# The last layer of a four-layer kernel: the fourth head's weights are turned by TensorE and copied by ScalarE, and unread bf16 products are set ahead of other products

## The chip, the cores and the metric

The kernel runs on one core of a Trainium2 chip. The core has engines with instruction streams of their own: PE (TensorE, matrix products; its weight loads are listed as PEld), DVE (VectorE), ACT (ScalarE), POOL (GpSimd) and SP (SyncE, which issues most DMAs here). PE writes to PSUM banks; DVE and ACT read them. The metric is the device time of one execution in microseconds, as the median of several runs.

## The reference

The input is x of 4 sequences by 1024 tokens by 128 features. Four layers each normalise x, apply a mixer and a feed-forward part, and add the product of the mixer's output and the silu of the other to x. Only the last layer's mixer matters here, attention with 16 heads of 8 features and learned relative distances:

```python
q, k, v = split_head(x @ Wq.T), split_head(x @ Wk.T), split_head(x @ Wv.T)
srel = srel_skew(einsum('bhnd,hmd->bhnm', q, e))      # e: embeddings by distance
qk = (einsum('bhnd,bhmd->bhnm', q, k) + srel) / sqrt(8)
atten = softmax(qk - mask)                             # causal
out = einsum('bhnm,bhmd->bhnd', atten, v) @ Wp.T + bp
```

With 1024 tokens and 256 embeddings, all farther distances share the first embedding. The feed-forward part of this layer is a gated one with 384 hidden features.

## The kernel before

`layer3` (L1736) holds the layer. Its 16 groups are 4 sequences by 4 sets i of 4 heads j. A group has 8 units, one for each tile t of 128 queries, in the order `ORDER3` = 7, 0, 6, 1, 5, 2, 4, 3 (L1733). A unit with tile t has (t + 1) x 128 keys, done in score tiles of up to 512 keys: one for t < 4, two for t > 3, so 12 score tiles a group and 192 in all.

**Scores** (`scores3`, L2077). The features of head j lie in rows 32j to 32j + 31, so a score product uses 32 of PE's 128 rows (L2097). Each score tile takes two PSUM tiles `halves`, heads 0 and 1 in one and heads 2 and 3 in the other, two banks each, from a pool of two such tiles (tag `sc`). DVE then reads them: it adds the distances `rel`, scales and finds the least value (L2113 for the up to five newest tiles of 128 keys, L2106 for older ones, where no distances are added), which frees the banks. ACT takes the exponential with the row's sum (L2120).

**Weights** (`transpose`, L1793). When all score tiles of a unit are compared, DVE turns the 4 heads' exponentials with a stream transpose (L1807), which turns each 32x32 block in its place, into `wT`. A unit with t > 3 is turned in two steps of two heads. Two units t = 2 pair and 2 pair + 1 share the buffers of a pair; there is one buffer for large t and one for small t, so that a new pair's transposes wait for the old pair's products.

**Weighted values** (`weigh3`, L2126). For blocks kb of 32 keys and each head, a product of `wT` with `vb` (L2134) adds to one PSUM tile `o`. Because of the 32x32 blocks, `vb` has the values placed so that each of four groups of 32 rows serves its own 32 queries. `values3` (L2009) loads the values in the layout of these blocks from DRAM, where `keep_values3` (L1886) put them, and POOL places them with four copies (L2018).

**Distances** (`relative3`, L2021). Two PSUM tiles `pr` for two heads take products of queries and embeddings (L2033); ACT copies them to `r` (L2035), and two DMAs on SP's queue write them to DRAM (L2038, L2039). `shear3` (L2042) reads them back shifted by row into `rel` and POOL masks them (L2064). The calls of `relative3` run 7 units ahead of their use, the reads about 3.

Beside it run, a step per unit, the feed-forward part (`ffn3`, L1972) of this sequence and the projections of the next sequence (`begin3`, L1933); the first sequence's are made during the third layer (`begin_first`, L1892). `finish3` (L2142) divides by the sums, `end3` (L2158) projects and stores. The tag `tr`, three banks, serves `pr`, `ffn3`, `begin3`, `finish3` and `end3`; tag `o` has one bank.

The program's main loop writes, for each score tile: the products of the next score tile, one waiting transpose, a step of the weighted values, the comparison of that next tile; and after a unit's last tile a call of `part` (distances), a step of project, of the parts beside, and `ahead` (the read of distances). A scheduler arranges each engine's instructions from this, by its own estimates, when the kernel is built; at run time each engine takes its own in order.

Of the kernel before, what the change touches and what calls it, by code (L numbers as in the profile page):

```python
# [10 lines left out]
F32 = mybir.dt.float32  # L11
BF16 = mybir.dt.bfloat16
# [8 lines left out]
P = 128  # L21
NB = 4
T = 1024
NT = 8
# [1711 lines left out]
def layer3(k, W, x3, out, eps5, ps, first):  # L1736
# [11 lines left out]
    nc, tc = k.nc, k.tc  # L1748
    with ExitStack() as st:
# [3 lines left out]
        for n in range(2):  # L1753
            q, kk = p1.tile([P, 1 + T], F32R, tag=f"q{n}", name="q"), p1.tile([P, T], F32R, tag=f"k{n}", name="k")
            nc.vector.memset(q[:, 0:1].bitcast(F32), 0.0)
            pairs.append((q, kk))
        vb = p1.tile([P, 32, 4, 4, 8], F32, tag="vb", name="vb")
        nc.gpsimd.memset(vb, 0.0)
        units = [(b, i, t) for b in range(NB) for i in range(4) for t in ORDER3]
        batch, group, flats, rels = {}, {}, {}, {}  # L1760

        def part(h):

            at, h = divmod(h, 8)
            if at < 4 * NB:
                pair = ORDER3[h // 4 * 4 + h // 2 % 2] // 2
                if h % 2 == 0:
                    flats[at, pair] = dram.tile([P, 4, 2, 384], F32, tag="flat", name="flat")
                relative3(k, W, temp, ps, flats[at, pair], group[at]["q"], at % 4, pair, h % 2)

        def ahead(n):
            if n < len(units):
# [2 lines left out]

        def stream():
            for n, (b, i, t) in enumerate(units):
                yield from scores3(k, p1, p2, ps, group[n // 8], rels.pop(n), t)

        batch[0] = {"qk": first["qk"], "vd": first["vd"], "xnT": p1.tile([P, T], F32, tag="xnT", name="xnT")}  # L1780
        nc.sync.dma_start(out=batch[0]["xnT"], in_=first["xnT"])
        group[0] = {}
        drain(project3(k, p2, pairs[0], batch[0], 0, group[0]))
        drain(values3(k, p1, batch[0], vb, 0))
# [8 lines left out]
        def transpose(n, heads):  # L1793

            b, i, t = units[n]
            at, pair = n // 8, t // 2
            big = t > 3
            if (at, pair) not in weights:
                for w in [w for w in weighs if w[0] == big]:
                    drain(w[1])  # L1800
                    weighs.remove(w)
                weights[at, pair] = [
                    p1.tile([P, 2, 1024 if big else 512], F32, tag=f"w{'b' if big else 's'}{j}", name="wT") for j in range(4)
                ]
            S = group[at]["S", t]
            for j in heads:
                nc.vector.transpose(weights[at, pair][j][:, t % 2, 0 : (t + 1) * P], S[j][:, 0 : (t + 1) * P])  # L1807
            if n % 8 in (2, 3, 6, 7) and heads[-1] == 3:
                weighs.append((big, weigh(n)))

# [28 lines left out]
        for x, (n, first) in enumerate(tiles + [(len(units), 0)] * 4):  # L1839
# [8 lines left out]
            b, i, t = units[n]  # L1848
# [34 lines left out]
        nc.sync.dma_start(out=rows[h], in_=a)  # L1883


def keep_values3(nc, to, v):  # L1886

    for a in range(4):
        nc.sync.dma_start(out=to[:, :, a], in_=v[32 * a : 32 * a + 32])


def begin_first(k, W, pool, ps, x, eps5, first):  # L1892
# [21 lines left out]
    for half in range(2):  # L1914
# [3 lines left out]
            nc.tensor.matmul(pv[:, t, :], xnT[:, at : at + P], W["WvT"], start=True, stop=True)  # L1918
        nc.scalar.copy(v[:, :, half * P : half * P + P].rearrange("p i (t d) -> p t i d", d=32), pv.rearrange("p t (i d) -> p t i d", d=32))
    keep_values3(nc, first["vd"], v)  # L1920
    yield


# [9 lines left out]
def begin3(k, W, p1, p2, temp, ps, dram, x3, b, eps5, seq):  # L1933
# [33 lines left out]
            yield  # L1967
    seq["vd"] = dram.tile([32, 4, 4, 256], F32, tag="vd", name="vd")
    keep_values3(nc, seq["vd"], v)


def ffn3(k, W, p1, temp, ps, seq):  # L1972
# [36 lines left out]
def values3(k, p1, seq, vb, i):  # L2009

    nc = k.nc
    v = p1.tile([P, 32, 32], F32, tag="vr", name="vr")
    at = seq["vd"][:, i]
    nc.sync.dma_start(out=v.rearrange("p n d -> p (n d)"), in_=bass.AP(at.tensor, at.offset, [(0, 4), (4096, 32), (1, 1024)]))
    yield
    for a in range(4):
        rows = slice(32 * a, 32 * a + 32)
        nc.gpsimd.tensor_copy(vb[rows, :, :, a, :], v[rows].rearrange("p n (j d) -> p n j d", d=8))  # L2018


def relative3(k, W, temp, ps, flat, q, i, pair, jp):  # L2021

# [2 lines left out]
    r = temp.tile([P, 2, 2, 256], F32, tag="temp", name="r")  # L2027
    js = (2 * jp, 2 * jp + 1)
    pr = [ps.tile([P, 2, 256], F32, tag="tr", name="pr") for _ in js]
    for m in range(2):  # L2030
        for j, to in zip(js, pr):
            at, t = slice(32 * j, 32 * j + 32), 2 * pair + m
            nc.tensor.matmul(to[:, m, :], q[at, t * P : (t + 1) * P], W["emb"][at, i, :], start=True, stop=True)  # L2033
# [40 lines left out]
    return rel  # L2074


def scores3(k, p1, p2, ps, group, rel, t):  # L2077

# [12 lines left out]
    for first in range(0, n, 512):  # L2093
        last = min(first + 512, n)
        halves = [ps.tile([P, 2, 512], F32, tag="sc", name="score") for _ in range(2)]
        for j in range(4):
            nc.tensor.matmul(  # L2097
                halves[j // 2][:, j % 2, 0 : last - first], q[at(j), 1 + t * P : 1 + n], kk[at(j), first:last], start=True, stop=True
            )
# [26 lines left out]
def weigh3(k, weights, vb, o, pair):  # L2126
# [4 lines left out]
    for n, kb in enumerate(groups):  # L2131
        m = slice(1, 2) if kb in second else slice(0, 2)
        for j in range(4):
            nc.tensor.matmul(  # L2134
                o[32 * j : 32 * j + 32, 2 * pair + m.start : 2 * pair + 2, :], vb[:, kb % 4 * NT + kb // 4, j].rearrange("p a d -> p (a d)"),
                weights[j][:, m, 32 * kb : 32 * kb + 32], start=(kb == 0), stop=(kb == both[-1]),
            )
        if pair > 1 and n + 1 in (len(groups) // 3, 2 * len(groups) // 3):
# [55 lines left out]
def tile_kernel(ctx: ExitStack, tc: tile.TileContext, I, out):  # L2194
# [9 lines left out]
    store = ctx.enter_context(tc.tile_pool(name="x3", bufs=1, space=DRAM))  # L2204
    x3 = store.tile([P, NB * NT, D], F32, tag="x3", name="x3")

    first = {name: store.tile(shape, F32, tag=name, name=name) for name, shape in (("qk", [2, 4, 4, 32, T]), ("vd", [32, 4, 4, 256]), ("xnT", [P, T]))}
    whole = ExitStack()
    xp = whole.enter_context(tc.tile_pool(name="x", bufs=1, side="right"))
    x_all = xp.tile([P, NB * NT, D], F32, tag="x_all", name="x_all")  # L2210
# [51 lines left out]
```

## Time and profile before

| | us |
|---|---|
| median of 3 runs (3174.36 to 3178.80) | 3178.16 |
| the profiled execution | 3175.99 |
| its span, first to last instruction | 3174.2 |
| first to last score product (the last layer's loop) | 985.5 |
| busy over the span: PE, DVE, ACT, POOL | 2163.6, 2291.8, 1542.6, 1167.5 |

A group's line names the line of the kernel, the engine, the operation, what it writes and reads, the shape and how often; then its busy time, the mean of one in ns, and after the bar the engine's idle time just before these instructions, with what ended it. A line of stretches gives a stretch of the span, then for each engine the busy time and the number of instructions in it, the mean granted TensorE clock (1 is full speed), the mean busy share of the 16 DMA engines, and GB/s. Matmuls are pipelined, so that the busy time of PE counts a product until its end, and products may overlap. Over the span's 40 slices the granted clock is 0.7 to 0.9 in the first eighteen, apart from one of 0.5, and 0.5 to 0.7 in the rest.

### The profile page before, as it was taken

How to read it: one execution, taken by the hardware profiler on the slowest of the kernel's cores; microseconds unless marked ns; L12 is line 12 of the kernel's file. 1: busy time of each engine (PE TensorE's matmuls, PEld its weight loads, DVE VectorE, ACT ScalarE, POOL GpSimd, SP SyncE). 2: the span in 40 equal slices, each digit the busy share in tenths (PEclk: the TensorE clock that was granted, in tenths of full speed). 3: DMA queues.
4: the chain of work that ended last, by engine and by line, in shares of the span. 5: the costliest groups of instructions: out<-in, count | busy, mean ns of one | idle time of the engine just before them, and what ended most of it. 6: DMA issues, size and time to landing. Idle time of an engine off the chain costs nothing. (4 is left out here: it accounts for less than half of the span.)

```text
span 3174.2 us, 47753 instructions
## 1 busy us (share of the span) xinstructions
PE 2163.6 (68%) x17039; PEld 1256.8 (40%) x17041; DVE 2291.8 (72%) x5558; ACT 1542.6 (49%) x3300; POOL 1167.5 (37%) x1094
## 2 busy tenths in 40 slices
PE   5777777577887776794543574375777777777865
PEld 2555555232332232562210122253544544544543
DVE  5554544878888786656778888676788797687777
ACT  3554544333333333535432463145765775775773
POOL 3433444144444434123477433232333332323322
PEclk9888888588888887895655566565766666766666
DMA  3000000100000000230334356339588588678772
GB/s 78 16 1 1 1 1 1 35 0 0 0 0 0 7 7 7 103 110 20 74 92 114 123 120 136 100 118 295 174 256 272 176 268 261 197 242 269 215 242 66
DMA packets 334065, 333.13 MB, mean 105 GB/s; under 512 B 25968, under 2 KB 307436, under 8 KB 328196
## 3 DMA queue, kind: packets, MB, share of 16 engines
q1 hardware_dynamic: 332676, 325.90, 34.6%
q10 hardware_dynamic: 1152, 4.19, 0.4%
q8 instruction: 134, 2.20, 0.3%
q14 instruction: 103, 0.84, 0.1%
HBM read 175.31 MB, written 154.14 MB: 104 GB/s over the span
## 5 line engine op out<-in xcount | busy, mean ns | idle before, releaser
L2120 ACT ACTIVATE neg<-neg,low 128x640 f32<-128x640 f32 (+7 forms) x512 | 390.7, 766 | 105.8 <-DVE low L2113 104.6
L1807 DVE STREAM_TRANSPOSE wT<-neg 128x640 f32<-128x640 f32 (+7 forms) x512 | 366.3, 754 | 50.3 <-PE po L2134 45.5
L2064 POOL TENSOR_SCALAR_AFFINE_SELECT rel<-rel 128x512 f32<-128x512 f32 x288 | 180.5, 638 | 551.4 <-DMA rel<-flat 412.6
L2134 PE MATMUL po<-wT,vb 128*32 128x64 f32 (+1 forms) x10240 | 266.2, 253 | 71.9 <-issue 40.8
L2097 PE MATMUL score<-k,q 32*128 32x512 f32 (+3 forms) x768 | 220.5, 587 | 124.6 <-DVE low L2113 121.3
L2134 PEld LDWEIGHTS po<-wT,vb 128*32 128x32 f32 x10240 | 210.9, 134 | 144.5 <-issue 84.1
L2113 DVE CUSTOM_DVE_ANT_0 neg<-score,rel,low 128x128 f32<-128x128 f32 (+3 forms) x448 | 213.0, 510 | 71.4 <-PE score L2097 29.3
L2035 ACT COPY r<-pr 128x512 f32<-128x512 f32 x256 | 135.2, 584 | 126.4 <-PE pr L2033 79.8
L2113 DVE CUSTOM_DVE_ANT_0 neg<-score,rel 128x512 f32<-128x512 f32 (+3 forms) x320 | 150.6, 520 | 50.4 <-POOL rel L2064 21.2
L2097 PEld LDWEIGHTS score<-k,q 32*128 32x128 f32 x768 | 96.8, 247 | 214.1 <-DVE low L2113 139.6
L837 PE MATMUL pg<-xnT,w 128*128 128x512 f32 x256 | 149.1, 666 | 7.1 <-DVE h L841 4.0
L2033 PE MATMUL pr<-emb,q 32*128 32x256 f32 x512 | 125.8, 426 | 39.7 <-ACT r L2035 25.5
L840 ACT ACTIVATE h<-pg 128x512 f32<-128x512 f32 x128 | 75.9, 596 | 157.5 <-PE pg L837 154.1
L790 POOL TENSOR_TENSOR prod<-rest,kv 128x2048 f32<-128x2048 f32 x32 | 145.5, 4598 | 18.4 <-ACT rest L780 18.4
L839 PE MATMUL pu<-xin,w 128*128 128x512 f32 x256 | 140.5, 632 | 12.9 <-DVE h L841 7.4
L828 PE MATMUL po<-h,w 128*128 128x512 f32 x256 | 129.8, 628 | 26.5 <-DVE h L841 26.5
L216 PE MATMUL pt<-ident,three 128*24 128x128 bf16 x64 | 9.2, 295 | 196.6 <-DVE three L213 196.6
L2033 PEld LDWEIGHTS pr<-emb,q 32*128 32x128 f32 x512 | 89.0, 262 | 74.4 <-ACT r L2035 38.9
L433 PE MATMUL px<-hT,xbcT 128*128 128x512 f32 x256 | 115.0, 593 | 0.0
L1086 PE MATMUL ph<-xin,upT 128*128 128x512 bf16 (+1 forms) x126 | 68.3, 572 | 66.4 <-DVE xin L1080 64.0
L1491 PE MATMUL read<-kt,const_sb 128*128 128x128 f32 x256 | 51.1, 372 | 90.3 <-POOL kt L1486 90.3
L785 DVE TENSOR_REDUCE s<-prod 128x128 f32<-128x2048 f32 x32 | 73.1, 2284 | 49.6 <-POOL prod L790 49.6
(633 smaller groups left out, 5775.7 us busy)
## 6 DMA issues: line engine op xcount, KB each, us to landing
flat<-r SPq DMA_DIRECT2D x128, 512.0 KB
rel<-flat SPq DMA_DIRECT2D x112, 512.0 KB
flat<-r SPq DMA_DIRECT2D x128, 256.0 KB
rel<-flat SPq DMA_DIRECT2D x96, 256.0 KB
kt<-kd SPq DMA_DIRECT2D x16, 512.0 KB
qt<-qd SPq DMA_DIRECT2D x16, 512.0 KB
kdc<-kdd SPq DMA_DIRECT2D x16, 512.0 KB
ktc<-ktd SPq DMA_DIRECT2D x16, 512.0 KB
```

The costliest lines, as they stand in the source:

```text
L790: nc.gpsimd.tensor_tensor(prod, attn.rearrange("p (t h g) -> p t h g", t=4, g=16)[:, t].unsqueeze(2).to_broadcast(each), kv[:, t, 1, :].re ...
L828: nc.tensor.matmul(po, W["w2"][:, e, c, :], h[:, c, :], start=(e == 0 and c == 0), stop=(e == 7 and c == 1))
L837: nc.tensor.matmul(pg, W["w1"][:, e, c * P : (c + 1) * P], xnT, start=True, stop=True)
L839: nc.tensor.matmul(pu, W["w3"][:, e, c * P : (c + 1) * P], xin, start=True, stop=True)
L1807: nc.vector.transpose(weights[at, pair][j][:, t % 2, 0 : (t + 1) * P], S[j][:, 0 : (t + 1) * P])
L2033: nc.tensor.matmul(to[:, m, :], q[at, t * P : (t + 1) * P], W["emb"][at, i, :], start=True, stop=True)
L2035: nc.scalar.copy(r[:, n], to)
L2064: nc.gpsimd.affine_select(out=rel[:, :, slot(back), :], in_=rel[:, :, slot(0), :], compare_op=op, fill=fill, base=0, pattern=[[0, 4], [-si ...
L2097: nc.tensor.matmul(halves[j // 2][:, j % 2, 0 : last - first], q[at(j), 1 + t * P : 1 + n], kk[at(j), first:last], start=True, stop=True)
L2113: nc.vector.tensor_tensor_reduce(out=neg[:, begin:last], in0=sc[:, begin - first : last - first], in1=rel[:, j, slot : slot + (last - begi ...
L2120: nc.scalar.activation(neg[:, 0:n], neg[:, 0:n], AF.Exp, bias=here, scale=-1.0, accum_out=group["sums"][:, j, t : t + 1])
L2134: nc.tensor.matmul(o[32 * j : 32 * j + 32, 2 * pair + m.start : 2 * pair + 2, :], vb[:, kb % 4 * NT + kb // 4, j].rearrange("p a d -> p (a ...
```

## The change

For j < 3 nothing changes in the transposes. For j = 3, PE transposes blocks of 128x128 (f32, by the identity) into a PSUM tile of tag `tr`, up to four blocks in one, and ACT copies that tile to `wT`. Since these blocks are turned whole, the fourth head's values need another placing: a second tile `vc` of 128 keys by block, query quarter and head feature, filled from `v3`, which for the first sequence goes through DRAM and for the others is copied by POOL. `vb` shrinks from four to three heads. The number and shapes of products in `weigh3` stay.

`beat` is a product of the bf16 identity with a tile of bf16 ones, 128x512, into a bank that the next real product writes anew, so that nothing reads it. It is set ahead of each half of a score tile (heads 0 and heads 2) and, in `relative3`, once for each of the two banks `pr`.

```diff
-        vb = p1.tile([P, 32, 4, 4, 8], F32, tag="vb", name="vb")
-        nc.gpsimd.memset(vb, 0.0)
+        vb = (
+            p1.tile([P, 32, 3, 4, 8], F32, tag="vb", name="vb"), p1.tile([P, NT, 4, 4, 8], F32, tag="vc", name="vc"),
+        )
+        for a in vb:
+            nc.gpsimd.memset(a, 0.0)
+        ones = p1.tile([P, 512], BF16, tag="ones16", name="ones")
+        nc.gpsimd.memset(ones, 1.0)
+
+        def beat(bank):
+            nc.tensor.matmul(bank, k.ident16, ones, start=True, stop=True)
...
+        batch[0]["v3"] = p2.tile([P, 4, NT, 8], F32, tag="v3", name="v3")
+        nc.sync.dma_start(out=batch[0]["v3"], in_=first["v3"])
...
             for j in heads:
-                nc.vector.transpose(weights[at, pair][j][:, t % 2, 0 : (t + 1) * P], S[j][:, 0 : (t + 1) * P])
+                to = weights[at, pair][j][:, t % 2]
+                if j < 3:
+                    nc.vector.transpose(to[:, 0 : (t + 1) * P], S[j][:, 0 : (t + 1) * P])
+                    continue
+                for begin in range(0, t + 1, 4):
+                    end = min(begin + 4, t + 1)
+                    pt = ps.tile([P, 4, P], F32, tag="tr", name="pt")
+                    for c in range(begin, end):
+                        nc.tensor.transpose(pt[:, c - begin, :], S[j][:, c * P : (c + 1) * P], k.ident)
+                    nc.scalar.copy(to[:, begin * P : end * P], pt[:, 0 : end - begin, :].rearrange("p c q -> p (c q)"))
...
+def fourth(v):
+    return v.rearrange("p i (t d) -> p i t d", d=32)[:, :, :, 24:32]
...  (begin_first)
+    nc.sync.dma_start(out=first["v3"], in_=fourth(v))
...  (begin3)
+    seq["v3"] = p2.tile([P, 4, NT, 8], F32, tag="v3", name="v3")
+    nc.gpsimd.tensor_copy(seq["v3"], fourth(v))
...  (values3)
-        nc.gpsimd.tensor_copy(vb[rows, :, :, a, :], v[rows].rearrange("p n (j d) -> p n j d", d=8))
+        nc.gpsimd.tensor_copy(vb[0][rows, :, :, a, :], v[rows].rearrange("p n (j d) -> p n j d", d=8)[:, :, 0:3])
+    for a in range(4):
+        nc.gpsimd.tensor_copy(vb[1][:, :, a, a, :], seq["v3"][:, i])
...  (relative3)
     pr = [ps.tile([P, 2, 256], F32, tag="tr", name="pr") for _ in js]
+    for to in pr:
+        beat(to.rearrange("p m u -> p (m u)"))
...  (scores3)
         for j in range(4):
+            if j % 2 == 0:
+                beat(halves[j // 2][:, 0])
             nc.tensor.matmul(
...  (weigh3)
-                o[32 * j : 32 * j + 32, 2 * pair + m.start : 2 * pair + 2, :], vb[:, kb % 4 * NT + kb // 4, j].rearrange("p a d -> p (a d)"),
+                o[32 * j : 32 * j + 32, 2 * pair + m.start : 2 * pair + 2, :],
+                (vb[0][:, kb % 4 * NT + kb // 4, j] if j < 3 else vb[1][:, kb // 4, kb % 4]).rearrange("p a d -> p (a d)"),
```

## The prediction

> **What bounds the kernel now.** I read the page's slices first, then the totals of the last layer's loop, then that loop in stretches of 10 us, then the waits of its lines, and last the granted clock window by window. The change touches the last layer alone; its loop of 192 score tiles runs from 2155.1 us to 3140.6 us, 985.5 us of the span of 3174.2 us.
>
> The totals of that loop (columns: busy time and instructions of each engine, mean granted TensorE clock, DMA share, GB/s):
>
> ```profile
> 2155.10:3140.60 985.50, 723.21 (x11750) 483.75 (x11750) 779.97 (x2535) 672.47 (x1512) 308.13 (x412) 0.68 0.76 233
> ```
>
> No engine is full: PE 73%, DVE 79%, ACT 68%, and the clock averages 0.68. The 10 us stretches show why; four of them:
>
> ```profile
> 2550.00:2560.00 10.00, 6.67 (x124) 4.16 (x120) 9.82 (x33) 4.97 (x10) 6.64 (x8) 0.90 1.08 372
> 2560.00:2570.00 10.00, 4.46 (x16) 2.04 (x16) 10.00 (x41) 4.61 (x14) 1.84 (x3) 0.50 1.02 294
> 2570.00:2580.00 10.00, 9.72 (x275) 7.69 (x279) 7.71 (x35) 9.31 (x18) 2.19 (x5) 0.58 0.71 194
> 2510.00:2520.00 10.00, 7.05 (x207) 5.53 (x205) 3.31 (x12) 9.88 (x18) 3.53 (x6) 1.00 0.70 202
> ```
>
> The lead changes. I took the busiest engine of each of the 97 stretches from 2160 us on. DVE leads in 52 (mean busy DVE 9.41, ACT 6.93, PE 6.70 us; clock 0.65), PE in 33 (6.09, 5.97, 8.28; 0.69), ACT in 12 (6.58, 9.09, 7.67; 0.76). The waits, by line, tie PE and DVE together:
>
> ```profile
> L1807 DVE STREAM_TRANSPOSE wT<-neg 128x640 f32<-128x640 f32 (+7 forms) x512 | 366.3, 754 | 50.3 <-PE po L2134 45.5
> L2097 PE MATMUL score<-k,q 32*128 32x512 f32 (+3 forms) x768 | 220.5, 587 | 124.6 <-DVE low L2113 121.3
> L2035 ACT COPY r<-pr 128x512 f32<-128x512 f32 x256 | 135.2, 584 | 126.4 <-PE pr L2033 79.8
> ```
>
> DVE spends 366 us turning weights, and waits 45.5 us there for the products that still read the old ones; PE waits 121 us for DVE to release score banks.
>
> The clock's record takes only the values 0.5 and 1.0 and changes at multiples of 3.41 us. Two successive windows, two more, and two from layer 2:
>
> ```profile
> 2503.37:2506.79 3.42, 3.42 (x21) 2.17 (x23) 1.35 (x7) 1.98 (x7) 1.57 (x3) 0.50 0.58 190
> 2506.79:2510.20 3.41, 3.41 (x53) 2.60 (x41) 1.72 (x7) 3.38 (x4) 0.73 (x1) 1.00 0.43 117
> 2517.03:2520.44 3.41, 0.11 (x2) 0.09 (x1) 0.55 (x2) 3.36 (x5) 2.11 (x4) 1.00 1.01 326
> 2520.44:2523.85 3.41, 3.41 (x17) 2.39 (x17) 0.00 (x0) 0.34 (x1) 1.23 (x2) 0.50 0.02 4
> ...
> 1547.64:1551.05 3.41, 3.19 (x14) 2.79 (x15) 0.50 0.85 202
> 1551.05:1554.46 3.41, 2.99 (x12) 0.89 (x10) 1.97 (x3) 2.97 (x7) 2.09 (x7) 1.00 0.69 147
> ```
>
> A window with much array work is followed by the full clock, one with little by half. For each window of the loop I counted columns streamed, an f32 column as two and a bf16 column as one (128 f32 columns start 111 ns apart at full clock, 512 bf16 columns 215 ns), times the share of array columns used, and left out products with 32 rows. Of 184 windows under 2,500, 6 were followed by full clock; of 74 at 3,000 or more, all. In the loop 33% of windows reach 2,600 and 36% run at full clock.
>
> **The change, part by part.** The sum is made against the profiled execution, 3175.99 us, 2.2 us below the median of 3178.16 us.
>
> *Transposes off DVE.* One of four per unit, 128 in all. The eight widths average 276 to 1232 ns and add to 6.03 us per group; 16 groups give 96.5 us, 12.4% of DVE's 780. In a DVE-led stretch that is 9.41 to 8.25 us.
>
> *Copies on ACT.* 192: 96 of 128x512 at 584 ns (the copy of products with distances), 32 each of 128, 256 and 384 columns. 256 columns took 376 ns (the copy of a group's output); the line through both gives 272 and 480. Sum 56.1 + 36.1 = 92 us, 13.7% of ACT's 672. In a DVE-led stretch ACT goes from 6.93 to 7.9 us, still below DVE; in an ACT-led one it adds up to 1.25 us where 0.91 is idle: +8 us over 12 stretches, between 0 and 15.
>
> *Transposes on PE.* 36 per group, 576. f32 transposes start 213 ns apart at half clock, 109 at full: 123 or 63 us.
>
> *Unread products.* Two per score tile (384) and two per call for distances (256): 640, each with its weight load. Nearest rows: bf16 128x512 with loads between, 308 to 320 ns apart at full and 537 at half; with loads hidden (24 rows), 215. So 138 to 202 us at full, up to 344 at half. A load needs no bank and may go ahead during the wait, which argues for the low end; I take the middle: 232 us for both additions at full clock, 2.36 us per 10 us.
>
> *The clock.* The products add 640 x 512 and the transposes 576 x 256 columns-worth, spread over 284 windows: 1,155 + 520. Added evenly, 62% of windows reach 2,600 instead of 33%. I take 0.70 of the time at full clock, since a PE with little idle time leaves fewer thin windows; the bounds are 0.45 (bunched, or PE waiting) and 0.85.
>
> [...] The window from 1547.64 us above holds 14 f32 transposes and hardly anything else, and the next ran at 1.00, so here they count. [...]
>
> *PE's sum.* At half clock the same work runs at 0.56 of full rate (109/213 for transposes, 493/791 for score products, medians). DVE-led: 6.70 us at 30% full is 4.64 us of full-clock work; the additions, in proportion to DVE's work (9.41 to a mean of 7.91), 2.8. Together 7.45, and at 0.70 full (rate 0.868) 8.58 us. That is above DVE's 8.25, so PE leads; with the 0.59 us idle of today's leader a stretch takes 9.17 instead of 10: 52 x 0.83 = -43 us. PE-led: 8.28 at 38% full is 6.02; additions 1.82; 9.03 us at the new clock, 0.75 more, of which I let half disappear in the 1.72 us idle: 33 x 0.37 = +12 us.
>
> *Waits.* The turned tiles use the three banks that products with distances also use, 12 more tiles a group beside their 16. PE waits for ACT's copies there about 0.15 us a bank today (25.5 us in 256 products' banks by the matmuls, 38.9 by the loads); 192 more give 29 us of PE wait, of which the PE-led third shows, +8. Queued behind that wait are the next score products, and DVE behind them; DVE's transposes cover it, and if they did not all 29 would show. On ACT the new copies wait for PE; the next unit's exponentials queue behind. The 45.5 us that DVE waits for old weights, the 51 for scores and 18 for the sums' product shrink with a faster PE: about -10, bounded by 0 and -20.
>
> *Edits at about nothing.* POOL fills two value tiles: four copies of 32x768 and four of 128x64 for four of 32x1024 (1,034 ns each), between -1 and +3 us a group. POOL is busy 31% and waits 412.6 us for distances to land; were that cover gone, it would be up to 48 us. One store (32-byte runs), one load and one fill at the layer's start, the load ahead of q and k on SP's queue: +1. No DMA is added per group.
>
> Sum: -43 + 12 + 8 + 8 - 10 + 1 = -24 us, about 0.8%; on the median some 3154 us.
>
> **Rivals.** (1) *The clock stays low and PE becomes the bound* (slower). For: full clock needs each window to be dense, and the unread products wait for the same bank as the scores, so they cannot fill PE's 121 us of waiting for DVE. Against: 62%. At 0.52 full (rate 0.789) DVE-led stretches take 9.44 + 0.59, +2 us in all; PE-led 9.94, of whose 1.66 more three quarters show, +41; with the +17 of the rest about +60 and, less the shrinking waits, 3178 + 55. It decides at 0.62 full, a granted clock of 0.81, where the sum is zero. (2) *Loads hide and the clock holds* (faster by more). At 0.85 full and 200 us of additions, PE needs 7.6 us in DVE-led stretches, so DVE's 8.25 leads: 8.84, -60; PE-led -6; the rest +7: 3119. For: once full, windows of 3,000 kept it in 52 of 52. Against: PE starves whenever DVE holds the banks. (3) *ACT or the landing of distances takes DVE's place* (no change): every DVE-led stretch stays at 10 us and only small terms remain, 3178 within 6 us. Against: ACT 7.9, DMA share 0.76.
>
> **How the numbers follow.** Forecast, 6 to 45 us faster: 0.38. Rival 2, more than that: 0.18. No change (0.2% is 6 us, about what a measurement of this kernel can tell): 0.08. Rival 1: 0.36. Faster 0.56, same 0.08, slower 0.36. The likeliest case alone spans 3133 to 3172. The range for 8 in 10 runs from 3100 (past rival 2, with ACT's +8 at zero and the waits at -20) to 3230 (rival 1).
>
> **What would show it.** Right: the loop's granted clock above 0.81; STREAM_TRANSPOSE x384 and about 96 us less DVE time; some 192 copies of about 480 ns on ACT; unread products 215 to 320 ns apart at full clock; DVE's wait for old weights below 45 us. Wrong: a clock under 0.8 with PE above 90% busy; exponentials waiting for PE's transposes; PE waiting for ACT's copies much beyond 60 us; DVE waiting longer for scores than 51 us.

## The result, and the profile after

The changed kernel takes 3289.59 us (median of 4 runs, 3287.22 to 3292.09) against 3178.36 us for the kernel before in the same session: ratio 1.0353, 95% interval 1.0335 to 1.0371. It is 111 us slower. I had forecast 3154 us. Nearly all of the difference lies in the last layer's loop, which grew from 985.5 to 1098.2 us; it starts 4 us later.

The loop in one stretch, first to last score product (as before: length, then busy time and instructions of PE, PE's loads, DVE, ACT and POOL, granted TensorE clock, DMA share, GB/s):

```profile
2159.50:3257.70 1098.20, 960.37 (x12940) 562.86 (x12939) 713.65 (x2410) 740.18 (x1690) 306.41 (x474) 0.79 0.69 208
```

PE is busy 960 us in place of 723, DVE 714 in place of 780, ACT 740 in place of 672. The clock rose from 0.68 to 0.79. Since the record holds only 0.5 and 1.0, that is 58% of the time at full clock in place of 36%. So the clock did rise and DVE was relieved; but only PE has less idle time in the loop than before, and DVE's went from 205 to 385 us.

The groups of the changed kernel (line, engine, operation, tiles, shapes, count; busy us, mean ns of one; idle time before them and its main cause):

```profile
L2154 ACT ACTIVATE neg<-neg,low 128x640 f32<-128x640 f32 (+7 forms) x512 | 391.8, 770 | 33.8 <-DVE low L2147 33.1
...
L2147 DVE CUSTOM_DVE_ANT_0 neg<-score,rel,low 128x128 f32<-128x128 f32 (+3 forms) x448 | 215.8, 515 | 150.2 <-PE score L2131 105.8
L1821 DVE STREAM_TRANSPOSE wT<-neg 128x1024 f32<-128x1024 f32 (+7 forms) x384 | 276.5, 756 | 56.0 <-PE po L2168 47.9
...
L1767 PE MATMUL score<-ones,ident 128*128 128x512 bf16 x384 | 179.0, 466 | 36.1 <-DVE low L2147 35.3
...
L1767 PE MATMUL pr<-ones,ident 128*128 128x512 bf16 x256 | 107.8, 464 | 30.3 <-ACT r L2067 17.3
L1828 ACT COPY wT<-pt 128x384 f32<-128x384 f32 (+1 forms) x192 | 86.7, 479 | 72.1 <-PE pt L1827 71.9
```

The prices of the moved work came out near my own: DVE's transposes fell from 366.3 to 276.5 us (-90; I had 96.5), ACT's 192 copies take 86.7 us at 479 ns (I had 92 and about 480). The unread products did not: the mean record is 466 ns. The comparison's line (L2113 before, L2147 after) tells what happened to DVE: 71.4 us of idle time before it became 150.2, led by PE's scores, 29.3 before and 105.8 now. The line before:

```profile
L2113 DVE CUSTOM_DVE_ANT_0 neg<-score,rel,low 128x128 f32<-128x128 f32 (+3 forms) x448 | 213.0, 510 | 71.4 <-PE score L2097 29.3
```

The same loop by waits (engine and line that waited, for whom; us in total, times, longest):

```profile
PEld score L2131 <- issue: 148.3, 373, 4.1
DVE neg L2147 <- PE score L2131: 128.6, 84, 11.2
ACT r L2067 <- PE pr L2065: 121.1, 62, 21.2
...
ACT wT L1828 <- PE pt L1827: 71.9, 76, 5.7
...
DVE neg L2140 <- PE score L2131: 51.1, 31, 15.1
...
DVE wT L1821 <- PE po L2168: 47.9, 18, 7.1
...
DVE neg L2147 <- ACT neg L2154: 39.5, 16, 4.7
...
PE score L1767 <- DVE low L2147: 35.3, 46, 3.6
...
DVE neg L2147 <- PE pt L1827: 22.9, 10, 4.8
```

The same waits in the kernel before:

```profile
PEld score L2097 <- issue: 58.1, 74, 2.1
...
DVE neg L2113 <- PE score L2097: 31.2, 23, 4.1
...
DVE neg L2106 <- PE score L2097: 20.1, 16, 9.3
```

DVE waits 180 us for scores (128.6 + 51.1; before 31.2 + 20.1). Before, PE waited 121 us for DVE to free score banks; now 35, and it is the unread product that waits. The score products wait instead behind it: their loads show 148 us of "issue", where no other engine holds them, 373 times (58 us and 74 times before). The 45.5 us that DVE waited for old weights did not shrink (47.9).

A stretch of the timeline shows the unread product in DVE's path (start, duration, engine, instruction, and in brackets the idle time before it with its cause):

```profile
2551.76 0.61 PE L1767 MATMUL score<-ones,ident 128*128 128x512 bf16 x1
...
2552.09 0.08 DVE L2140 DVE_READ_ACCUMULATOR neg<-score 128x1 f32 x1
2552.30 0.29 PEld L2131 LDWEIGHTS score<-k,q 32*128 32x128 f32 x2 [0.43 <-issue]
2552.30 0.79 PE L2131 MATMUL score<-k,q 32*128 32x512 f32 x2
...
2553.23 0.29 DVE L2140 TENSOR_SCALAR_CACHE_REDUCE neg<-score 128x128 f32<-128x128 f32 x1 [1.06 <-PE score L2131]
```

DVE is done at 2552.17 and has nothing to compare. PE starts the unread product at 2551.76, the load of the first score product only at 2552.30, and DVE starts at 2553.23, 1.06 us idle. The clock is at half here (0.50), as it mostly is when DVE waits for scores: of the 180 us, 109 lie in windows at half clock, which make up 42% of the loop.

### The profile page after: what moved, and what is told of

Its sections match the earlier page's. It is cut to its first block, busy times and chain, and to the rows that moved or that the text cites. A ratio compares the mean times of both kernels' runs of the same rounds, so it can differ in the third digit from the quotient of the medians.

```text
span 3290.4 us, 50230 instructions
## 1 busy us (share of the span) xinstructions
PE 2409.9 (73%) x18257; PEld 1338.7 (41%) x18257; DVE 2223.9 (68%) x5430; ACT 1613.2 (49%) x3484; POOL 1168.4 (36%) x1163
## 5 line engine op out<-in xcount | busy, mean ns | idle before, releaser
L2147 DVE CUSTOM_DVE_ANT_0 neg<-score,rel,low 128x128 f32<-128x128 f32 (+3 forms) x448 | 215.8, 515 | 150.2 <-PE score L2131 105.8
L1821 DVE STREAM_TRANSPOSE wT<-neg 128x1024 f32<-128x1024 f32 (+7 forms) x384 | 276.5, 756 | 56.0 <-PE po L2168 47.9
L2168 PE MATMUL po<-wT,vb 128*32 128x64 f32 (+1 forms) x7680 | 219.4, 238 | 28.8 <-issue 22.8
L2147 DVE CUSTOM_DVE_ANT_0 neg<-score,rel 128x512 f32<-128x512 f32 (+3 forms) x320 | 154.3, 523 | 111.7 <-ACT neg L2154 39.5
L1767 PE MATMUL score<-ones,ident 128*128 128x512 bf16 x384 | 179.0, 466 | 36.1 <-DVE low L2147 35.3
L2168 PEld LDWEIGHTS po<-wT,vb 128*32 128x32 f32 x7680 | 178.3, 124 | 64.4 <-issue 41.1
L2131 PE MATMUL score<-k,q 32*128 32x512 f32 (+3 forms) x768 | 203.4, 516 | 0.1
L2168 PE MATMUL po<-wT,vc 128*32 128x64 f32 (+1 forms) x2560 | 190.6, 238 | 9.1 <-issue 8.9
L2168 PEld LDWEIGHTS po<-wT,vc 128*32 128x32 f32 x2560 | 164.5, 124 | 22.2 <-issue 17.5
L1827 PE MATMUL pt<-const_sb,neg 128*128 128x128 f32 x576 | 125.2, 356 | 14.0 <-ACT neg L2154 5.9
L1767 PE MATMUL pr<-ones,ident 128*128 128x512 bf16 x256 | 107.8, 464 | 30.3 <-ACT r L2067 17.3
L1828 ACT COPY wT<-pt 128x384 f32<-128x384 f32 (+1 forms) x192 | 86.7, 479 | 72.1 <-PE pt L1827 71.9
```

Source lines behind the costliest of these rows:

```text
L1767: nc.tensor.matmul(bank, k.ident16, ones, start=True, stop=True)
L1821: nc.vector.transpose(to[:, 0 : (t + 1) * P], S[j][:, 0 : (t + 1) * P])
L2131: nc.tensor.matmul(halves[j // 2][:, j % 2, 0 : last - first], q[at(j), 1 + t * P : 1 + n], kk[at(j), first:last], start=True, stop=True)
L2147: nc.vector.tensor_tensor_reduce(out=neg[:, begin:last], in0=sc[:, begin - first : last - first], in1=rel[:, j, slot : slot + (last - begi ...
L2168: nc.tensor.matmul(o[32 * j : 32 * j + 32, 2 * pair + m.start : 2 * pair + 2, :], (vb[0][:, kb % 4 * NT + kb // 4, j] if j < 3 else vb[1][ ...
```

## The experiments

Eighteen kernels ran, in five sessions; each ratio is against the kernel before on the same chip. "Score wait" is DVE's wait for score products in the loop, "full" the share of the loop at full clock (twice the granted clock, less one).

| run | edit | us | ratio, 95% interval | loop us | full | PE, DVE busy us | score wait us |
|---|---|---|---|---|---|---|---|
| before | | 3178 | 1 | 985.5 | 0.36 | 723, 780 | 51 |
| after | the change | 3289.6 | 1.0353 (1.0335 to 1.0371) | 1098.2 | 0.58 | 960, 714 | 180 |
| e1 | after, no unread products | 3226.9 | 1.0149 (1.0119 to 1.0179) | 1041.2 | 0.37 | 813, 708 | 113 |
| e2 | before, with unread products | 3232.2 | 1.0168 (1.0137 to 1.0199) | 1039.6 | 0.52 | 919, 785 | 105 |
| e8 | e2 with 128 columns | 3217.4 | 1.0129 (1.0100 to 1.0158) | 1021.7 | 0.37 | 874, 785 | 88 |
| e5 | before, DVE relieved | 3150.2 | 0.9924 (0.9901 to 0.9946) | 964.8 | 0.33 | 729, 705 | 63 |
| e6 | before, with unread turns | 3187.5 | 1.0030 (1.0008 to 1.0051) | 1000.4 | 0.40 | 792, 784 | 59 |
| e7 | before, with unread copies | 3160.8 | 0.9949 (0.9934 to 0.9964) | 972.3 | 0.35 | 713, 781 | 34 |
| e10 | e5 and e6 | 3158.2 | 0.9933 (0.9914 to 0.9951) | 967.9 | 0.45 | 774, 707 | 71 |
| e13 | e10 and whole copies | 3203.6 | 1.0079 (1.0063 to 1.0095) | 1010.7 | 0.41 | 815, 711 | 75 |
| e14 | e1, copies unread | 3183.0 | 1.0020 (1.0008 to 1.0032) | 993.4 | 0.45 | 787, 708 | 67 |
| e16 | before, products bunched | 3211.6 | 1.0104 (1.0091 to 1.0117) | 1023.7 | 0.32 | 711, 782 | 61 |
| e17 | before, products spread | 3205.6 | 1.0080 (1.0067 to 1.0093) | 1021.5 | 0.33 | 737, 785 | 75 |
| e18 | e1, products lagging | 3242.4 | 1.0194 (1.0176 to 1.0213) | 1060.3 | 0.41 | 858, 713 | 118 |

**The two halves of the change.** e1 takes the two `beat` calls out of the changed kernel, e2 puts them alone into the kernel before.

```diff
# e1, against after
-    for to in pr:
-        beat(to.rearrange("p m u -> p (m u)"))
...
-            if j % 2 == 0:
-                beat(halves[j // 2][:, 0])
# e2, against before: the same four lines added, with ones and beat
```

> The changed kernel without its 640 unread products; the fourth head is still turned by PE and copied by ACT. Theory A (the unread products fill PE: they took 237 us of PE's own time in the loop of the changed kernel, and the faster clock gave back less): PE's time falls from 960 us to about 780, the loop's granted clock from 0.79 to about 0.72, DVE's wait for scores from 180 us to about 70, and the time is 3165 to 3215 us. Theory B (the turning on PE is what costs, by the shared banks and by ACT's queue): 3250 us or more, with DVE still waiting over 120 us for scores. Theory C (each part alone fits into PE's idle time, only both together fill it): 3185 us or less.

> The kernel before with the 640 unread products alone; DVE turns all four heads. Theory A: PE's time rises from 722 us to about 850, the granted clock from 0.68 to 0.76 or more, and the time is 3230 to 3290 us. Theory B: 3178 us or less, since the clock is faster and nothing else is in the way. Theory C: within 30 us above 3178.

Both halves lose on their own: the turning 48 us (3226.9 against 3179.2 in that session), the unread products 53, and their sum of 101 is near the 111 of both. The clock that the unread products bring is real (e2: 52% at full clock in place of 36%), but what it gives back is less than what they take. Counted from each product's start to the next start on PE (or to its own end, if PE is idle then), the unread products take 252 us of e2's loop, 0.40 us each, while all of PE's work together grew by 196 (722 to 918): the rest of it, at the faster clock, became 56 us shorter.

**Where the unread products stand.**

```diff
# e3, against after: ahead of score halves only
-    for to in pr:
-        beat(to.rearrange("p m u -> p (m u)"))
# e4, against after: ahead of products with distances only
-            if j % 2 == 0:
-                beat(halves[j // 2][:, 0])
```

> The changed kernel with the 384 unread products ahead of half score tiles alone, none ahead of products with distances. Theory A by PE time (150 of the 237 us): between the run without any and the changed kernel, nearer the latter: about 3250 us. If it is their place that matters, between DVE's release of the banks and the scores that DVE waits for: nearly all of the loss, 3275 us or more.

> The changed kernel with the 256 unread products ahead of products with distances alone. Theory A by PE time (87 of the 237 us): about 3225 us. If it is the place ahead of scores that matters: within 15 us of the run without any unread product.

e3 took 3256.2 us (1.0244, 1.0200 to 1.0288) and e4 3264.7 us (1.0271, 1.0230 to 1.0311). Above e1 that is 29 us for 384 products and 38 us for 256, together 67 where both at once cost 63. So no place among the two is harmless, and they add up. Those ahead of the distances look dearer, 0.148 us of time each against 0.076, but by two runs each, with intervals of some 14 us to either side.

**Array time or the mere instruction.**

```diff
# e8, against e2
-            nc.tensor.matmul(bank, k.ident16, ones, start=True, stop=True)
+            nc.tensor.matmul(bank[:, 0:128], k.ident16, ones[:, 0:128], start=True, stop=True)
```

> The kernel before with the 640 unread products ahead of the same products, each of 128 columns in place of 512. If their streaming time is what costs (0.40 us each with 512 columns in the run with unread products alone, 53 us slower): a quarter to a third of the loss, 3190 to 3200 us, and a granted clock of the loop near 0.70. If a weight load and an issue in front of the scores cost as much: 3215 us or more.

A quarter of the columns still costs 40 of e2's 53 us. The loop of e2 as one stretch, first to last score product, in the columns used above:

```profile
2159.56:3199.15 1039.59, 918.64 (x12373) 503.66 (x12372) 784.78 (x2536) 674.80 (x1510) 306.94 (x411) 0.76 0.71 219
```

And of e8:

```profile
2155.31:3177.01 1021.70, 873.95 (x12381) 557.58 (x12380) 784.83 (x2535) 677.06 (x1512) 307.92 (x412) 0.68 0.73 224
```

With 128 columns the clock is not lifted (0.68), and PE is still busy 874 us. By starts, the short products themselves take 117 us, the score products 212 in place of 188 and those with distances 136 in place of 104: at half clock one of the latter goes from 239 to 347 ns. The starts show where this comes from. Before, 1006 of the score and distance products, which use 32 rows each, are followed on PE by another of them, after 161 ns on average counted as above, and 503 of these starts come within 50 ns, where a score product's record lasts 587 ns on average: such products overlap. In e8, 365 of them are followed by an unread product, which uses all rows; it never starts sooner than 202 ns after, on average 431 ns. So the price is the interruption as much as the 512 columns, and it stays when the clock's gain is gone.

**The turning, part by part.** Unread transposes on PE, unread copies on ACT, and DVE relieved of its transposes with nothing in their place:

```diff
# e5, against before (fourth head's products read the third head's turned weights)
+                if j < 3:
+                    nc.vector.transpose(weights[at, pair][j][:, t % 2, 0 : (t + 1) * P], S[j][:, 0 : (t + 1) * P])
-                nc.vector.transpose(weights[at, pair][j][:, t % 2, 0 : (t + 1) * P], S[j][:, 0 : (t + 1) * P])
...
-                weights[j][:, m, 32 * kb : 32 * kb + 32], start=(kb == 0), stop=(kb == both[-1]),
+                weights[min(j, 2)][:, m, 32 * kb : 32 * kb + 32], start=(kb == 0), stop=(kb == both[-1]),
# e6, against before: for j == 3 also
+                    pt = ps.tile([P, 4, P], F32, tag="tr", name="pt")
+                    for c in range(begin, end):
+                        nc.tensor.transpose(pt[:, c - begin, :], S[j][:, c * P : (c + 1) * P], k.ident)
# e7, against before: for j == 3 also
+                    spare = p1.tile([P, 512], F32, tag="spare", name="spare")
+                    nc.scalar.copy(spare[:, 0 : (end - begin) * P], S[j][:, begin * P : end * P])
```

> The kernel before without the fourth head's stream transposes, and nothing in their place: the products with the fourth head's values read the third head's turned weights, so the fourth head's result is left out. This is the gain that was to be had from DVE alone. If DVE's own time bounds the loop, about 96 us less of it shows for the most part: 3090 to 3120 us. If the ties between PE and DVE bound it: 3130 us or more.

> The kernel before, and beside it PE transposes the fourth head's blocks (576 of them) into the same three banks, where nobody reads them; DVE still turns all four heads. This is the cost of PE's part alone. If scores queue behind PE's added time of some 130 us: 3225 us or more. If that time falls into PE's 263 us of waiting: 3190 us or less, and the loss of the turning lies with ACT's copies and the banks held for them.

> The kernel before, and beside it ACT copies the fourth head's exponentials to a spare tile that nobody reads, 192 copies of the same widths. This is the cost of ACT's part alone, about 90 us of ACT time. If ACT has room (it is busy 672 of 985 us): 3190 us or less. If exponentials and copies of distances queue behind: 3215 us or more.

Taking 75 us of work off DVE saved 27 (3150.2 against 3177.0). DVE's time without work in the loop grew from 205 to 260 us: the wait for POOL's distances from 44 to 63, for scores from 51 to 63. PE's transposes cost 10 us. ACT's copies cost less than nothing, -16: no work was taken away in e7, so this gain must come from how the rest is arranged by the build's scheduler and falls in time, which was not tried apart. The three sum to -33, while all of them together cost +48, with the link that the change has: the fourth head's products read ACT's copies and the second value tile. That gap of 81 us was the open question.

**Banks.** My first explanation was that turned tiles hold the three `tr` banks until ACT, in order behind its exponentials, copies them.

```diff
# e9, against e6: the bank is held until ACT gets to it
+                    spare = p1.tile([P, 4, 1], F32, tag="spare", name="spare")
+                    nc.scalar.copy(spare[:, 0 : end - begin], pt[:, 0 : end - begin, 0:1])
# e12, against before
-        ps = PsumTags(st, tc, {"sc": 2, "tr": 3, "o": 1}, "ps3")
+        ps = PsumTags(st, tc, {"sc": 2, "tr": 2, "o": 1}, "ps3")
```

> The kernel before with PE's 576 transposes of the fourth head added unread (the earlier run of that: 1.003), and after each of the 192 turned tiles a copy of one column per block on ACT, so that a bank is free again only when ACT, in order, gets to it. DVE's own transposes stay and are the ones used. Theory that the turning's loss is a bank held until ACT reaches it behind its exponentials: 3215 us or more, ratio above 1.012, ACT waiting 40 us or more for PE's transposes. Theory that the loss comes from PE's work and the absent transposes on DVE, and not from holding banks: 3180 to 3200 us, ratio 1.001 to 1.007.

> The kernel before with two banks in place of three for products with distances and the stages beside; nothing else. If the loop is sensitive to these banks: 3215 us or more, ratio above 1.012, and then turned tiles that hold them longer must cost. If not: 3178 us within 12, and bank sharing falls as the turning's price.

e9: 3191.7 us, 1.0036 (1.0019 to 1.0053), against e6's 1.0030. e12: 3182.3 us, 1.0011 (0.9998 to 1.0024). Neither holding banks nor having one less shows a price above some 10 us. ACT did wait for PE's transposes in e9 as I had said it would; its waits (the profiled execution is one of the shorter of e9's, which go from 3175.9 to 3199.0 us):

```profile
ACT spare L1816 <- PE pt L1814: 73.2, 76, 4.3
...
DVE neg L2115 <- PE score L2106: 29.9, 13, 8.9
...
DVE neg L2122 <- PE score L2106: 24.1, 23, 2.6
```

73 us of ACT's waiting there, as much as the 72 in the changed kernel, and DVE's wait for scores stays at 54 us. The theory of banks falls, and so does the wait that I read as its sign.

**Relief, turns, copies, link, one after the other.**

```diff
# e10: e5 and e6 together
# e13, against e10
+                    spare = p1.tile([P, 512], F32, tag="spare", name="spare")
+                    nc.scalar.copy(spare[:, 0 : (end - begin) * P], pt[:, 0 : end - begin, :].rearrange("p c q -> p (c q)"))
# e14, against e1: copies and second value tile are written, but not read
-                (vb[0][:, kb % 4 * NT + kb // 4, j] if j < 3 else vb[1][:, kb // 4, kb % 4]).rearrange("p a d -> p (a d)"),
-                weights[j][:, m, 32 * kb : 32 * kb + 32], start=(kb == 0), stop=(kb == both[-1]),
+                vb[0][:, kb % 4 * NT + kb // 4, min(j, 2)].rearrange("p a d -> p (a d)"),
+                weights[min(j, 2)][:, m, 32 * kb : 32 * kb + 32], start=(kb == 0), stop=(kb == both[-1]),
# e11, against e1: copies on DVE
-                    nc.scalar.copy(to[:, begin * P : end * P], ...)
+                    nc.vector.tensor_copy(to[:, begin * P : end * P], ...)
# e15, against before: values in two tiles, three heads and one
-        nc.gpsimd.tensor_copy(vb[rows, :, :, a, :], v[rows].rearrange("p n (j d) -> p n j d", d=8))
+        for to, heads in zip(vb, (slice(0, 3), slice(3, 4))):
+            nc.gpsimd.tensor_copy(to[rows, :, :, a, :], v[rows].rearrange("p n (j d) -> p n j d", d=8)[:, :, heads])
```

> The kernel before without DVE's transposes of the fourth head and with PE's 576 transposes of it, unread; no copies on ACT. The fourth head's products read the third head's turned weights, so its result is left out. Alone the two edits gave 0.9924 and 1.003. Additive theory: 3160 us, ratio 0.993 to 0.998, and what the turning loses comes in with ACT's copies. Theory that PE's transposes and DVE's relief work against each other (the score tile freed by PE, which is late, and no more by DVE): 3195 us or more, ratio above 1.006, DVE waiting over 90 us for scores and for PE's transposes together.

> The run with DVE's relief and PE's unread transposes (ratio 0.9933) with the 192 copies on ACT added, whole tiles into one spare tile that nothing reads; values filled as before; the fourth head's products still read the third head's turned weights, so its result is left out. Theory that ACT's copies, waiting in order for PE with exponentials behind them, make the turning's loss: 3210 us or more, ratio above 1.010. Theory that the loss needs the products that read ACT's tile, or the two value tiles: 3150 to 3180 us, ratio below 1.001.

> The changed kernel without its 640 unread products (ratio 1.0149), where the fourth head's products read the third head's turned weights and values, so that nothing reads ACT's copies or the second value tile, which are still written; the fourth head's result is left out. Theory of ACT's copies: no change, 3215 to 3235 us, ratio 1.011 to 1.018. Theory that the loss lies in PE waiting in order for ACT's turned tile before the products: below 3185 us, ratio below 1.002. Theory of the values' new copies on POOL: no change from 1.0149 either, and the run of the values alone shows the loss.

> The changed kernel without its 640 unread products (ratio 1.0149), with the 192 copies of turned tiles on DVE in place of ACT. DVE's busy time then is about that of before (192 copies of 128 to 512 columns, at most the 96 us of the transposes they replace). Theory that the loss is ACT waiting in order for PE's transposes, with exponentials behind: 3180 to 3200 us, ratio below 1.008, though DVE is no lighter. Theory that the loss is the three banks shared with distances and the stages beside: 3215 us or more, ratio above 1.012, with PE waiting for copies as before.

> The kernel before with the values in two tiles, three heads and one, filled by eight copies on POOL instead of four; nothing else. I costed this edit at -1 to +3 us a group with POOL's waits for distances as cover, 0 in the sum. If that holds: 3178 us within 16, the size by which small edits moved the loop so far. If POOL's copies are the turning's loss: 3210 us or more, ratio above 1.010.

Relief and turns add (e10: 0.9933). With whole copies on ACT behind PE's transposes the gain is gone: 25 us above before in e13, 4 in e14, where the copies go to the real tile. With the link to the products, e1, it is 48. So whole copies cost 24 to 45 us on top of e10, and the link another 23 to 44, each in the order that its build got. That the copies must wait for PE isn't shown to be the reason: e9's short copies waited as long, 73 us, and cost 2 to 4. The waits of DVE (us in total, times, longest), first in e1:

```profile
DVE neg L2143 <- PE score L2127: 80.9, 42, 9.0
...
DVE neg L2143 <- ACT neg L2150: 53.1, 18, 4.7
DVE wT L1821 <- PE po L2164: 53.0, 19, 8.2
...
DVE neg L2136 <- PE score L2127: 32.4, 18, 9.2
```

and then in e14:

```profile
DVE neg L2143 <- PE score L2127: 36.1, 37, 2.9
...
DVE neg L2136 <- PE score L2127: 30.8, 19, 9.2
...
DVE wT L1821 <- PE po L2164: 29.8, 10, 7.9
...
DVE neg L2143 <- ACT neg L2150: 19.2, 15, 2.1
```

With nothing but the reading products put on the real tile, DVE waits 46 us longer for scores, 34 longer for exponentials and 23 longer for old weights. None of these is a wait for the link itself: it shows up second hand, in what PE and ACT do in another order or later. Copies on DVE (e11: 3213.5 us, 1.0110, 1.0088 to 1.0132) put the work back where it was and still lose 35, so the loss isn't a matter of ACT alone. The values in two tiles cost nothing (e15: 3177.7 us, 0.9995, 0.9985 to 1.0006), as predicted, though e15 leaves out the second tile's other layout.

**The order of the products.** With the link, PE's instructions are arranged in another way: of the 5120 products of weighted values, 2036 stand in runs of more than 100 without a score product between them in e1, 904 in e14, 529 before. I took that for the cause and made such runs longer and shorter without adding or taking away work.

```diff
# e16, against before (e17: pair > 0 in place of pair > 1)
-        if pair > 1 and n + 1 in (len(groups) // 3, 2 * len(groups) // 3):
-            yield
+    yield
# e18, against e1: the fourth head's products six key blocks behind
+    order = [(n, j) for n in range(len(groups) + 6) for j in range(4) if 0 <= (n if j < 3 else n - 6) < len(groups)]
...
+        kb = groups[n if j < 3 else n - 6]
...
+        if pair > 0 and at + 1 in [len(order) * a // 4 for a in (1, 2, 3)]:
+            yield
```

> The kernel before with the two breaks in the products of the weighted values taken out, so that a pair's products go on in one step; no work is added or taken away. In the order on PE, runs of more than 100 of these products without a score product between hold 1410 of the 5120, against 529 before, 2036 in the changed kernel without unread products and 904 in the same without the link from copies to products. Theory that the turning's loss is in long runs of these products ahead of the scores that DVE waits for: 3200 to 3225 us, ratio 1.007 to 1.015, DVE waiting over 70 us for scores (51 before). Theory that the order of these products does not matter: 3178 us within 16.

> The kernel before with the two breaks also in the products of the second smallest pair of tiles; no work is added or taken away. Runs of more than 100 products without a score product between hold 160 of 5120 (529 before; 160 also in the run with 192 unread copies on ACT, ratio 0.9949). Theory of long runs: 3155 to 3172 us, ratio 0.993 to 0.998, and this is a version that beats both kernels. Theory that the order does not matter: 3178 us within 16, on either side.

> The changed kernel without its 640 unread products (ratio 1.0149), with the fourth head's products six key blocks behind the other heads', and three breaks in place of two, from the second smallest pair on. Runs of more than 100 products without a score product between hold 1394 of 5120 in place of 2036. Theory of long runs: 3195 to 3215 us, ratio 1.005 to 1.012. Theory that the order does not matter: 3227 us within 16.

e16 fits in its time, though DVE waits 61 us for scores and not over 70; e17 and e18 go the other way: shorter runs, and slower by 26 us against before and by 15 against e1. And e7 and e17 have the same 160 products in long runs, with times some 40 us apart. The length of the runs, as I counted them, does not explain the loss. What the pair does show is more useful. The loop of e16 as one stretch:

```profile
2152.11:3175.84 1023.73, 711.24 (x11752) 478.51 (x11752) 782.26 (x2534) 677.67 (x1516) 307.84 (x412) 0.66 0.76 224
```

And of e17:

```profile
2151.87:3173.40 1021.53, 736.72 (x11751) 493.57 (x11750) 784.57 (x2534) 682.27 (x1519) 307.38 (x412) 0.66 0.75 225
```

PE, DVE and ACT do the work of before, to within 14 us of busy time; yet the loop is 38 and 36 us longer and the clock lower, 0.66. The place is the same in both: from one group's last product of weighted values to the next group's, the groups of the third set take 66 and 65 us on average in place of 57. The next sequence begins to be prepared beside them; but the last sequence's third group, which has none to prepare, is longer too (61 and 59 us in place of 52), so that this isn't the whole reason. An edit that makes the scheduler arrange the work anew, then, moved the time by -16 (e7, which only adds work) to +32 us (e16) without any work being dearer. In e15, where the products stand in runs of the same lengths as before, the time stayed too.

So the turning's 48 us are placed thus far, each step in the order that its build got: DVE's relief gives 27, PE's transposes take back 3 to 10, banks and values next to nothing, and the copies with their link take 68. How much of the 68 are waits that any order would have, and how much is the order, stays open: the effect of order alone, up to 32 us, is of the size of each of the two steps (copies 24 to 45, link 23 to 44). The smaller steps are no safer. PE's order changed in them too (892 products in long runs in e5), and their 3 to 27 us are less than order alone moved. It changed in e2 as well (631), so that a part of the 53 us of the unread products may be order, though not all of it if 32 is the most that order does.

## Why the prediction was wrong, step by step

Three steps failed: the price of the additions on PE (232 us at full clock; 278 by starts), the share of full clock (0.70; 0.58), and the term for waits (-10 us; DVE's wait for scores alone grew by 129). The first two are enough to turn the forecast's sign.

*Confirmed.* The sizes of the moved work on DVE and ACT; the values at nothing; the wait for `tr` banks as a small matter (my +8; e9 against e6 shows 2, e12 at most 8); transposes on PE that do count for the clock (full clock for 45% of the loop in e10 against 33% in e5, which differ by the transposes and the order that came with them).

*The price of the additions* ("I take the middle: 232 us for both additions at full clock"). By starts, an unread product takes 0.32 us ahead of scores and 0.28 ahead of distances at full clock, 0.53 and 0.49 at half; a transpose 0.145 and 0.23. At full clock that sums to 384 x 0.317 + 256 x 0.282 + 576 x 0.145 = 278 us, at the clock of the run to 237 + 106 = 343. The argument for the low end was that a load goes ahead during the wait. Loads did: of the 62 unread products for which PE stood idle over 0.2 us, 35 had their load done at least 0.1 us before they started (the one at 2361.99 us 3.16 us before). Yet the low end failed: at full clock, by the median, the next start comes 319 ns after an unread product ahead of scores and 309 after one ahead of distances, as in the prediction's row with loads between (308 to 320 ns); and a transpose took 0.145 us on average in place of 0.109. What an unread product does to the 32-row products ahead of it (e8) was no term of the sum at all. The prediction's row with hidden loads has 215 ns at full clock; between other products, the starts here are 282 to 317 ns apart on average.

*The clock* ("I take 0.70 of the time at full clock"). It was 0.58, below the 0.62 at which my rival 1 said the sum turns; the granted clock of 0.79 is below its 0.81. The estimate of 62% of windows was near; the step up to 0.70, that a busier PE leaves fewer thin windows, was the error. In the turning alone the clock hardly moved (e1: 0.37).

*The sum with these two put right.* Full share 0.58 gives a rate of 0.58 + 0.42 x 0.56 = 0.815. DVE-led stretches: (4.64 + 2.8 x 278/232)/0.815 + 0.59 = 10.4 us, 52 x 0.41 = +21. PE-led: (6.02 + 1.82 x 278/232)/0.815 = 10.06, 1.78 more, three quarters of it over 33 stretches +44. With +7 for the rest: +72, some 3250 us. So two mis-sized terms turn the sign and make 96 of the 136 us by which I was off, and this is rival 1. The 39 us that are left I put down to what this kind of sum doesn't hold, waits and the order; no run takes them apart.

*The missing part: waits* ("about -10, bounded by 0 and -20"). The term had the wrong sign. DVE's wait for scores went from 51 to 180 us, for old weights from 45.5 to 47.9, and two waits are all but new: 40 us for exponentials (1.4 on that line before) and 23 for PE's transposes, which by the record of waits still read an exponentials' tile that DVE is to write anew. I added work to the leading engine of a stretch; but scores, comparison and release of a bank follow each other in a ring, and an instruction set ahead of the score product lengthens the ring whoever leads. This is how I read the waits: putting the unread products into the kernel before raised DVE's wait for scores from 51 to 105 us (e2). I had written of this in rival 1 ("they cannot fill PE's 121 us of waiting for DVE") and put no price on it.

*The relief of DVE.* "In a DVE-led stretch that is 9.41 to 8.25 us" stood for 52 stretches, 60 us if nothing else led; alone it was worth 27 (e5): of the 75 us by which DVE's work shrank in the profiled execution, 55 came back as idle time of DVE, waiting for POOL's distances, scores and ACT.

*The order.* I took the arrangement as given. e16 and e17 show that it is worth as much as the effect I forecast, 32 and 26 us against 24.

## What to carry to other kernels

Products that only keep the clock up can cost time when they stand ahead of products that another engine waits for: 640 of them took 53 us here although the clock rose from 0.68 to 0.76. Both places tried lost; whether they would pay where nothing waits for PE was not tried. Where several engines sit at 70 to 80% and wait for one another in a ring, work taken off the busiest one need not come back in full: 75 us off DVE gave 27, and the parts of the turning did not add once they were linked. And where a scheduler arranges the instructions, run an edit that changes no work beside the one you study: here that alone moved the time by 0.8 and 1.0% (e16, e17), and an edit that only added work made it 0.5% shorter (e7).

## What the hardware showed that I had not expected

Short full-array products did not come cheap beside 32-row products: 128 bf16 columns, set 640 times, cost 40 us, and in e8 an unread product never started within 202 ns of the 32-row product ahead of it, where half of the 32-row products that follow one another start within 50 ns. Transposes added to the loop raised its time at full clock (0.36 to 0.40 in e6, 0.33 to 0.45 from e5 to e10). In e10, PE's busy time in the loop is only 45 us above e5's, for transposes that take 119 by starts: the rest of PE's work became 74 us shorter, of which the faster clock makes some 53 by the prediction's 0.56 at half clock (an estimate). And the clock's mean says little of the moments that count: at 0.58 full in the changed kernel, 109 of the 180 us that DVE waited for scores lay in windows at half clock.
